# The start of a routed two-stage FFN kernel: first tile transposed uncentred, its row lookup taken ahead, and another order of gathers and matrix loads

## The chip, the cores and the metric

The kernel runs on one core of a Trainium2 chip. The metric is the device time of one execution in microseconds. TensorE is called PE here, VectorE DVE, ScalarE ACT, GpSimd POOL and SyncE SP, as in the profile. POOL issues the indirect DMAs (gathers and scatters of rows), SP the plain ones.

## The reference

2048 tokens of 512 numbers pass through two residual blocks. In the first one each token belongs to one of four experts by its id, and each expert has one 512x512 matrix, used for all three products:

```python
x = x + tanh(g_xattn[0]) * xattn(layernorm(x), ids, ctx, ctx, ctx)
x = x + tanh(g_ffn[0]) * ffn(layernorm(x), w1, w3, w2, wr)

def xattn(h, ids, Wg, Wu, Wd):           # per token's expert e
    e = minimum(clip(ids, 0, 24999) // 6250, 3)
    return (silu(h @ Wg[e].T) * (h @ Wu[e].T)) @ Wd[e].T

def ffn(x, w1, w3, w2, wr):
    gates, idx = top-2 of softmax(x @ wr.T), normalised
    h = silu(silu(x @ w1.T) @ w3.T) @ w2.T
    out = zeros_like(x)
    for k in range(2): out = out.at[idx[:, k]].add(gates[:, k:k+1] * h)
```

Wg, Wu and Wd are the same tensor, so z = h @ W.T is needed once, g = silu(z) * z, and y = g @ W.T. The second block adds into 8 rows only (the 8 routes), which is why its output is small.

## The kernel before

**Sorting the tokens.** The tokens are sorted by expert into 17 tiles ("passes") of 128 rows: 13 tiles that belong to one expert each (NF), and 4 mixed tiles in four groups of 32 rows. The list `order` gives the order in which they are worked. Lines 183 to 253 turn the ids into a place for every token: its tile (`inpass`) and its row in the tile (`lanes`). Lines 265 and 273 (`at_lane`) build one-hot matrices `atlane` (128 x 128 for each of 16 groups of tokens, the first 12 groups in one DVE instruction, the last 4 in another). Lines 266 to 272 build `what`, which holds for each of the 17 tiles the token's number where the token falls into that tile. 16 PE products (line 276) of the two give `tok`: for each row of each tile the number of its token. `from_row` (line 286) is the list of rows to gather, one column a tile. `which` (lines 287 to 300) tells for each tile the expert's offset in the matrices; `which0` (line 245) is the same for the first tile alone and is ready earlier. `row_tables()` (line 305) makes `to_row`, the rows to scatter to, and `first`, used much later.

`busy(n)` (line 198) issues n PE products of ones whose result nobody reads; there are 10 before the lookup and 21 behind it.

**Work on a tile.** `gather(p)` has POOL fetch the tile's rows x_p by an indirect DMA. `load(p)` has SP read the expert's offset from SBUF (`look_up`) and issue the 1 MB matrix load. `centre(p)` has DVE compute mean and variance (BATCH_NORM_STATS, BATCH_NORM_AGGREGATE) and h = x - mean. `scale(p)` has DVE compute 1/sqrt(variance) in nine small operations. `turn_in(p)` transposes h on PE (four 128x128 transposes) and copies it to SBUF on ACT (hT). `up(p)`: eight PE products z = hT x matrix, ACT's silu with the scale, DVE's product g (line 467). `turn_mid(p)` transposes g and copies it (gT). `down(p)`: eight PE products y, DVE's x + tanh(gate) * y in place (line 481), POOL's scatter to the output. `norms` and `turn_out` prepare the second block's input. For the first tile `first_in` stands in place of centre and turn_in: the same in two halves of 256 columns, so that PE and ACT can start on the first half.

**What sets the order.** Each engine works its instructions in the program's order, written out by hand (`manual_schedule`), and waits on semaphores for the others. The text at lines 836 to 874 is therefore the order of the start on each engine:

- DVE: the lookup, `row_tables`, first_in(0), scale 0, centre 1, scale 1, [g of tile 0], centre 2, scale 2, [g of tile 1], centre 3.
- POOL: gather 0, a copy of one entry of `which` into `held` (line 849), gathers 1 to 4, a copy of all later entries into `held` (line 854), then scatters and gathers in turn.
- SP: load 0 (offset from which0), load 1 (waits for the first copy into `held`), load 2 (waits for the second), the two gates, load 3, load 4, load 5, w1, wr and so on.
- PE: lookup, the 21 products of `busy`, transposes of tile 0, z_0 with the transposes of tile 1 put ahead of its last two products, z_1 with the transposes of g_0 ahead of its last two, the transposes of tile 2, y_0, the transposes of g_1, z_2.

Since SP reads the offsets of load 1 and on from `held`, such a load is issued only behind the gathers that stand ahead of its copy on POOL. Matrix tiles have 7 buffers, x tiles 5, hT 2, h 4.

Of the kernel before, what the change touches and what calls it, by code (L numbers as in the profile page):

```python
# [19 lines left out]
P = 128  # L20
# [5 lines left out]
def tile_gated_moe_ffn(  # L26
# [68 lines left out]
    positions = ExitStack()  # L95
    pos = positions.enter_context(tc.tile_pool(name="pos", bufs=1))
    on_the_way = {
        "lane", "atlane12", "atlane4", "passes", "what", "place", "over", "rank_in", "incl",
        "keep", "cum", "hot", "before", "later", "stepped", "behind", "ones", "place0", "number",
        "idt", "pad", "psum", "padded", "lanes", "inpass",  # L100
    }
# [30 lines left out]
    whole = ct_([P, 2, E], I32, "whole")  # L132
    nc.vector.memset(whole[:, 0, :], -P)
    nc.vector.memset(whole[:, 1, :], -Q)
    cut = ct_([P, 2 * E + 1], F32, "cut")
    nc.vector.memset(cut, 0.0)
    bounds = ct_([P, E - 1], F32, "bounds")
    for e in range(1, E):
        nc.vector.memset(bounds[:, e - 1 : e], BOUNDS[e - 1])

    steps = ct_([P, 2 * E - 1], F32, "steps")
# [6 lines left out]
        out=before, in_=before, pattern=[[-1, P]], compare_op=ALU.is_ge,  # L148
        fill=0.0, base=0, channel_multiplier=1,
    )  # L150
    H = 12
    lane = ct_([P, P, H], I16, "lane")
    nc.gpsimd.iota(lane, pattern=[[1, P], [0, H]], base=0, channel_multiplier=0)
    passes = ct_([P, NP, NJ], I16, "passes")
    nc.gpsimd.iota(passes, pattern=[[P, NP], [0, NJ]], base=0, channel_multiplier=0)

    number = ct_([P, NJ], F16, "number")
    nc.gpsimd.iota(
        number, pattern=[[1, NJ]], base=1, channel_multiplier=NJ,
# [3 lines left out]
    NU = NF + (NP - NF) * G  # L163
# [9 lines left out]
    ident = ct_([P, P], F32, "ident")  # L173
# [30 lines left out]
    incl = ct_([P, E, NJ], F32, "incl")  # L204
# [18 lines left out]
    rank_in = ct_([P, E, NJ], F32, "rank_in")  # L223
# [8 lines left out]
    over = ct_([P, E, NJ], F32, "over")  # L232
# [18 lines left out]
    nc.vector.tensor_single_scalar(lanes, padded, P - 1, op=ALU.bitwise_and)  # L251
    inpass = ct_([P, NJ], I16, "inpass")
    nc.vector.tensor_single_scalar(inpass, padded, -P, op=ALU.bitwise_and)
    atlane = [ct_([P, P, n], F16, f"atlane{n}") for n in (H, NJ - H)]

    def at_lane(h):
        j, n = (0, H) if h == 0 else (H, NJ - H)
        return nc.vector.tensor_tensor(
            atlane[h],
            lane[:, :, 0:n],  # L260
            lanes[:, j : j + n].unsqueeze(1).to_broadcast([P, P, n]),
            ALU.is_equal,
        )

    at_lane(0)
    what = ct_([P, NP, NJ], F16, "what")
    nc.vector.tensor_tensor(
        what, passes, inpass.unsqueeze(1).to_broadcast([P, NP, NJ]), ALU.is_equal
# [1 line left out]
    nc.vector.tensor_tensor(  # L270
        what, what, number.unsqueeze(1).to_broadcast([P, NP, NJ]), ALU.mult
    )
    at_lane(1)
    tok = ps_x.tile([P, NP], F32, tag="x", name="tok")
    for j in range(NJ):
        nc.tensor.matmul(
            tok, atlane[j // H][:, :, j % H], what[:, :, j], start=(j == 0), stop=(j == NJ - 1)
        )

    which = ct_([P, NU], I32, "which")  # L280
    later = ct_([P, 2 * E, NU], F32, "later")
    stepped = ct_([P, 2 * E - 1, NU], F32, "stepped")

    busy(21)
    from_row = ct_([P, NP], I32, "from_row")
    nc.vector.tensor_scalar(from_row, tok, -1.0, 0.0, ALU.add, ALU.max)
    nc.vector.tensor_tensor(
# [17 lines left out]
    def row_tables():  # L305

        pad = ct_([P, NP], F32, "pad")
        nc.vector.tensor_scalar(pad, tok, 1.0, float(4 * NT), ALU.is_lt, ALU.mult)
        nc.vector.scalar_tensor_tensor(to_row, tok, -1.0, pad, ALU.add, ALU.add)

        pads = ct_([P, E], F32, "pads")
        nc.vector.tensor_sub(pads, size[:, 2, :], num[:, 0, :])
        behind = ct_([P, E, NU - NF], F32, "behind")
        nc.vector.tensor_tensor(
            behind,
            later[:, E : 2 * E, NF:NU],
            pads.unsqueeze(2).to_broadcast([P, E, NU - NF]),
            ALU.mult,
        )
        psum = ct_([P, NU - NF], F32, "psum")  # L320
        nc.vector.tensor_reduce(psum, behind.rearrange("p e n -> p n e"), AX.X, ALU.add)
        nc.vector.tensor_sub(psum, place0[:, NF:NU], psum)
        nc.vector.tensor_scalar(
            first, psum, float(-(NB - 1) * TB), float(TB), ALU.add, ALU.min
        )
# [61 lines left out]
    def gather(p):  # L387
        xt = xp.tile([P, D], F32, tag="x", name=f"x_{p}")
        nc.gpsimd.indirect_dma_start(  # L389
            out=xt,  # L390
            out_offset=None,
            in_=x,
            in_offset=bass.IndirectOffsetOnAxis(ap=from_row[:, p : p + 1], axis=0),
        )
# [16 lines left out]

    def first_in(p):

        st = small.tile([P, 6], F32, tag="st", name=f"st_a{p}")
        nc.vector.bn_stats(st, xs[p])
        mvs[p] = small.tile([P, 2], F32, tag="mv", name=f"mv_a{p}")
        nc.vector.bn_aggr(mvs[p], st)
        hTs[p] = work.tile([P, KC * P], F32, tag="hT", bufs=2, name=f"hT_{p}")
        n = D // 2
        for i in range(2):  # L420
            h = work.tile([P, n], F32, tag="h", bufs=4, name=f"h_a{p}_{i}")
            nc.vector.tensor_scalar(
                h, xs[p][:, i * n : (i + 1) * n], mvs[p][:, 0:1], None, ALU.subtract
            )
            tp = ps_tp.tile([P, n], F32, tag="tp", name=f"tp_a{p}_{i}")
            for k in range(n // P):
                nc.tensor.transpose(tp[:, k * P : (k + 1) * P], h[:, k * P : (k + 1) * P], ident)
            nc.scalar.copy(hTs[p][:, i * n : (i + 1) * n], tp)  # L428
# [32 lines left out]
    def up(p, inside=None):  # L461
        z = ps_mm.tile([P, D], F32, tag="mm", name=f"z_{p}")
        expert_product(z, hTs.pop(p), p, inside)
        g = work.tile([P, D], F32, tag="g", bufs=2, name=f"g_{p}")
        rs = rss.pop(p)
        nc.scalar.activation(g, z, AF.Silu, scale=rs)  # L466
        nc.vector.scalar_tensor_tensor(g, z, rs, g, ALU.mult, ALU.mult)  # L467
        gs[p] = g

    def turn_mid(p):  # L470
        tp = transposed(gs.pop(p), f"g{p}")
        gT = work.tile([P, KC * P], F32, tag="gT", bufs=2, name=f"gT_{p}")
        nc.scalar.copy(gT, tp)  # L473
        gTs[p] = gT
# [358 lines left out]
            if r in (0, SHORT):  # L833
                step()

    row_tables()
    positions.close()
    ffp = ctx.enter_context(tc.tile_pool(name="ffp", bufs=1))
    held = ct_([P, NU], I32, "held")

    def look_up(i):
# [1 line left out]

    load(order[0])
    gather(order[0])
    one = slice(order[1], order[1] + 1)
    nc.gpsimd.tensor_copy(held[0:1, one], which[0:1, one])
    load(order[1])  # L850
    for i in range(1, 5):
        gather(order[i])
    rest = slice(order[1] + 1, NU)
    nc.gpsimd.tensor_copy(held[0:1, rest], which[0:1, rest])
    first_in(order[0])
    scale(order[0])
    centre(order[1])
    scale(order[1])
    load(order[2])
    nc.sync.dma_start(gates[:, 0:1], g_xattn.to_broadcast([P, 1]))  # L860
    nc.sync.dma_start(gates[:, 1:2], g_ffn.to_broadcast([P, 1]))
    load(order[3])
    up(order[0], inside=lambda: turn_in(order[1]))
    centre(order[2])
    scale(order[2])
    up(order[1], inside=lambda: turn_mid(order[0]))
    turn_in(order[2])
    centre(order[3])
# [94 lines left out]
```

## Time and profile before

| | us |
|---|---|
| median of three runs (lowest, highest) | 279.38 (278.96, 279.59) |
| profiled execution | 277.53 |
| its span, first to last instruction | 275.8 |
| PE busy | 266.6 (97%) |
| DVE busy | 148.7 (54%) |
| ACT busy | 69.3 (25%) |
| POOL busy | 39.3 (14%) |

How to read it: the span is cut by what the engines did, and a busy share of 97% says that PE is the bound nearly everywhere; the idle rest is at the start. The granted TensorE clock is 1.00 throughout. The chain of work that ended last is followed back from the last instruction; a name of a DMA in it is time from issue to landing. In the timeline, a line has start, duration, engine, line of the kernel, operation, output <- inputs, shape and count; in brackets stands the idle time of the engine ahead of it and what ended that. Neighbouring instructions of one line are merged into one line of the timeline.

The first 35 us go thus: the ids land at 2.56, the lookup products end about 8.9, gather 0 is issued at 9.35 and has landed at 12.87, matrix 0 is issued at 6.13, matrix 1 at 11.16, matrix 2 at 16.25. z_0 starts at 15.44, z_1 at 19.47, y_0 at 23.85, z_2 at 27.73.

### The profile page before, as it was taken

How to read it: one execution, taken by the hardware profiler on the slowest of the kernel's cores; microseconds unless marked ns; L12 is line 12 of the kernel's file. 1: busy time of each engine (PE TensorE's matmuls, PEld its weight loads, DVE VectorE, ACT ScalarE, POOL GpSimd, SP SyncE). 2: the span in 40 equal slices, each digit the busy share in tenths (PEclk: the TensorE clock that was granted, in tenths of full speed). 3: DMA queues.
4: the chain of work that ended last, by engine and by line, in shares of the span. 5: the costliest groups of instructions: out<-in, count | busy, mean ns of one | idle time of the engine just before them, and what ended most of it. 6: DMA issues, size and time to landing. Idle time of an engine off the chain costs nothing.

```text
span 275.8 us, 3562 instructions
## 1 busy us (share of the span) xinstructions
PE 266.6 (97%) x1173; PEld 125.4 (45%) x1173; DVE 148.7 (54%) x593; ACT 69.3 (25%) x134; POOL 39.3 (14%) x63
## 2 busy tenths in 40 slices
PE   5889999999999999999999999999999999999994
PEld 2445455544355454444344444534245444344362
DVE  6677877777888769918263481516253620711000
ACT  2022232232232231223143232312113233311120
POOL 6520122221122211211110010101010000000000
PEclk9999999999999999999999999999999999999999
DMA  0697998545669996697304084001000000000000
GB/s 1 217 354 277 408 402 334 173 155 206 228 225 402 389 409 258 173 398 264 112 26 166 2 312 180 38 0 40 0 12 2 0 0 1 0 0 2 0 0 2
DMA packets 20722, 42.54 MB, mean 154 GB/s; under 512 B 2143, under 2 KB 2207, under 8 KB 20704
## 3 DMA queue, kind: packets, MB, share of 16 engines
q1 hardware_dynamic: 17952, 33.66, 34.0%
q0 software_dynamic: 2720, 8.65, 8.3%
q8 instruction: 9, 0.15, 0.2%
q14 instruction: 9, 0.07, 0.1%
q10 hardware_dynamic: 32, 0.01, 0.0%
HBM read 38.10 MB, written 4.47 MB: 154 GB/s over the span
## 4 chain that ended last, share of the span: by engine, by line
PE 94%; DVE 2%; DMA 2%; issue 1%; ACT 0%; DVEq 0%
PE z L453 22%; PE y L453 21%; PE v L730 20%; PE X L622 10%; PE Y L622 5%; PE tp_f L380 3%; PE tp_a L380 3%; PE tp_g L380 3%; PE Z L622 2%; PE acc L742 1%; PE lg L699 1%; DMA x<-in_x_dram,from_row 1%; DMA idt<-in_ids_dram 1%; PE accT L758 1%; PE o L814 0%
## 5 line engine op out<-in xcount | busy, mean ns | idle before, releaser
L453 PE MATMUL z<-m,hT 128*32 128x512 f32 (+1 forms) x232 | 61.8, 595 | 0.2 <-ACT hT L428 0.2
L453 PE MATMUL y<-m,gT 128*32 128x512 f32 (+1 forms) x232 | 61.4, 594 | 0.0
L730 PE MATMUL v<-w,s 128*128 128x512 f32 (+1 forms) x136 | 57.3, 570 | 0.0
L730 PEld LDWEIGHTS v<-w,s 128*128 128x128 f32 x136 | 25.0, 190 | 27.2 <-issue 26.7
L453 PEld LDWEIGHTS z<-m,hT 128*32 128x32 f32 (+1 forms) x232 | 22.6, 146 | 29.5 <-issue 28.1
L453 PEld LDWEIGHTS y<-m,gT 128*32 128x32 f32 (+1 forms) x232 | 22.6, 146 | 27.8 <-issue 27.8
L482 POOL DMA_INDIRECT out_dram<-x,to_row x17 | 17.2, 1011 | 84.9 <-DVE x L481 82.7
L389 POOL DMA_INDIRECT x<-in_x_dram,from_row x17 | 16.7, 984 | 77.5 <-DVE h_a L401 22.9
L467 DVE SCALAR_TENSOR_TENSOR g<-z,rs_a,g 128x512 f32<-128x512 f32 x17 | 12.7, 750 | 27.1 <-ACT g L466 27.0
L466 ACT ACTIVATE g<-z,rs_a 128x512 f32<-128x512 f32 x17 | 11.7, 687 | 51.3 <-PE z L453 51.3
L481 DVE SCALAR_TENSOR_TENSOR x<-y,tg,x 128x512 f32<-128x512 f32 x17 | 12.7, 749 | 16.9 <-PE y L453 16.8
L738 ACT ACTIVATE s<-v 128x512 f32<-128x512 f32 (+1 forms) x17 | 9.7, 572 | 41.9 <-PE v L730 41.9
L515 ACT COPY hT<-tp_f 128x512 f32<-128x512 f32 x13 | 7.6, 587 | 43.5 <-PE tp_f L380 43.5
L340 DVE BATCH_NORM_STATS2 st_a<-x 128x6 f32<-128x512 f32 x16 | 11.0, 688 | 7.5 <-DMA x<-in_x_dram,from_row 7.5
L622 PE MATMUL X<-T,S 128*128 128x512 f32 x32 | 15.0, 592 | 0.0
L380 PEld LDWEIGHTS tp_f<-ident,h_f 128*128 128x128 f32 x68 | 8.2, 141 | 10.2 <-issue 10.2
L340 DVE BATCH_NORM_STATS2 st_f<-x 128x6 f32<-128x512 f32 x17 | 11.8, 695 | 0.6
L380 PEld LDWEIGHTS tp_a<-ident,h_a 128*128 128x128 f32 x64 | 7.7, 140 | 9.4 <-issue 9.1
L640 DVE TENSOR_TENSOR s<-X,c 128x512 f32<-128x512 f32 x4 | 2.8, 692 | 16.2 <-PE X L622 16.2
L473 ACT COPY gT<-tp_g 128x512 f32<-128x512 f32 x17 | 10.0, 586 | 5.3 <-PE tp_g L380 5.3
L380 PE MATMUL tp_f<-ident,h_f 128*128 128x128 f32 x68 | 10.4, 276 | 0.0
L380 PE MATMUL tp_g<-ident,g 128*128 128x128 f32 x68 | 10.2, 273 | 0.0
(165 smaller groups left out, 271.6 us busy)
## 6 DMA issues: line engine op xcount, KB each, us to landing
m<-in_ctxT_dram SPq DMA_DIRECT2D x29, 1024.0 KB
w<-in_w1T_dram SPq DMA_DIRECT2D x1, 1024.0 KB
w<-in_w3T_dram SPq DMA_DIRECT2D x1, 1024.0 KB
w<-in_w2T_dram SPq DMA_DIRECT2D x1, 1024.0 KB
x<-in_x_dram,from_row POOLq DMA_INDIRECT x17, 6.2
out_dram<-x,to_row POOLq DMA_INDIRECT x17, 6.1
wr<-in_wrT_dram SPq DMA_DIRECT2D x1, 64.0 KB
x_first<-out_dram SPq DMA_DIRECT2D x4, 4.0 KB
```

What stands on the lines that cost most here:

```text
L340: nc.vector.bn_stats(st, xt)
L380: nc.tensor.transpose(tp[:, k * P : (k + 1) * P], h[:, k * P : (k + 1) * P], ident)
L389: nc.gpsimd.indirect_dma_start(out=xt, out_offset=None, in_=x, in_offset=bass.IndirectOffsetOnAxis(ap=from_row[:, p : p + 1], axis=0),)
L453: nc.tensor.matmul(out_ps[i * n : (i + 1) * n, :], lhs[:, k * P + i * n : k * P + (i + 1) * n], m[:, k, :], start=(k == 0), stop=(k == KC ...
L466: nc.scalar.activation(g, z, AF.Silu, scale=rs)
L467: nc.vector.scalar_tensor_tensor(g, z, rs, g, ALU.mult, ALU.mult)
L473: nc.scalar.copy(gT, tp)
L481: nc.vector.scalar_tensor_tensor(xt, y, tg[:, 0:1], xt, ALU.mult, ALU.add)
L482: nc.gpsimd.indirect_dma_start(out=out, out_offset=bass.IndirectOffsetOnAxis(ap=to_row[:, p : p + 1], axis=0), in_=xt, in_offset=None, bou ...
L622: nc.tensor.matmul(out_ps, a[:, k, c * P : (c + 1) * P], bb[:, k, :], start=start and k == 0, stop=k == 1, skip_group_check=True,)
L730: nc.tensor.matmul(v, s1[:, k, c_b + t * P : c_b + (t + 1) * P], w3[:, k, c0 : c0 + n], start=(k == 0), stop=(k == KC - 1),)
L738: nc.scalar.activation(s2, v, AF.Silu)
```

## The change

1. *Lookup of the first tile ahead.* The one-hot matrices are built in three instructions of 6, 6 and 4 groups instead of two of 12 and 4. A column `what0` for the first tile alone is made first, and 16 products of one column each give `tok0`, from which `from_row0` is made; only then come `what` for all tiles and the 16 full products. `which1` (the second tile's offset) is made from the cuts directly, as which0 was. `busy` has 3 products behind the first lookup and 10 behind the second.
2. *First tile transposed as it comes.* `first_in` transposes x_0 itself instead of x_0 - mean. The mean is subtracted afterwards: DVE sums each row (`total`), a PE product spreads the sums along the transposed tile's columns (`spread`, in PSUM), and DVE computes hT = raw - spread / 512 in two halves. Mean and variance of tile 0 follow on DVE.
3. *Another order of gathers and loads.* Gather 0 reads `from_row0`; gathers 1 and 2 read `from_row`; all later ones read `rows_on`, a copy of it that DVE makes behind `first_in`. POOL's copy for load 1 stands behind gather 0 as before, now with `which1`; the copy for all later loads stands behind gather 2 instead of gather 4.
4. *Another order on DVE.* centre 1 stands ahead of scale 0, centre 2 ahead of g_0, scale 1 and scale 2 behind g_0, and `row_tables` behind scale 2 and ahead of g_1.

```diff
-    H = 12
+    H = 6
...
+    what0 = ct_([P, NJ], F16, "what0")
+    nc.vector.scalar_tensor_tensor(what0, inpass, 0.0, number, ALU.is_equal, ALU.mult)
+    at_lane = []
+    for i, j in enumerate(range(0, NJ, H)):
+        n = min(H, NJ - j)
+        at = ct_([P, P, n], F16, f"atlane{i}")
+        nc.vector.tensor_tensor(
...
+            ALU.is_equal,
+        )
+        at_lane.extend(at[:, :, k] for k in range(n))
+    tok0 = ps_x.tile([P, 1], F32, tag="x", name="tok0")
+    for j in range(NJ):
+        nc.tensor.matmul(
+            tok0, at_lane[j], what0[:, j : j + 1], start=(j == 0), stop=(j == NJ - 1)
+        )
+    busy(3)
+
+    start1 = ct_([P, 2 * E - 1], F32, "start1")
+    nc.vector.scalar_tensor_tensor(
+        start1, cut[:, 1 : 2 * E], float(P), steps, ALU.is_le, ALU.mult
+    )
+    which1 = ct_([P, 1], I32, "which1")
+    with nc.allow_low_precision("whole numbers below 4096"):
+        nc.vector.tensor_reduce(which1, start1, AX.X, ALU.add)
+    from_row0 = ct_([P, 1], I32, "from_row0")
+    nc.vector.tensor_scalar(from_row0, tok0, -1.0, 0.0, ALU.add, ALU.max)
...
-    busy(21)
+    busy(10)
...
-            in_offset=bass.IndirectOffsetOnAxis(ap=from_row[:, p : p + 1], axis=0),
+            in_offset=bass.IndirectOffsetOnAxis(
+                ap=from_row0
+                if p == order[0]
+                else (from_row if p in order[1:3] else rows_on)[:, p : p + 1],
+                axis=0,
+            ),
...
-        st = small.tile([P, 6], F32, tag="st", name=f"st_a{p}")
-        nc.vector.bn_stats(st, xs[p])
...
+        raw = work.tile([P, KC * P], F32, tag="h", bufs=4, name=f"raw_{p}")
         for i in range(2):
...
+                nc.tensor.transpose(tp[:, k * P : (k + 1) * P], xs[p][:, c : c + P], ident)
+            nc.scalar.copy(raw[:, i * n : (i + 1) * n], tp)
+        total = small.tile([P, 1], F32, tag="total", name="total")
+        nc.vector.tensor_reduce(total, xs[p], AX.X, ALU.add)
+        spread = ps_y.tile([P, P], F32, tag="y", name="spread")
+        nc.tensor.matmul(spread, total.to_broadcast([P, P]), ident, start=True, stop=True)
+        hTs[p] = work.tile([P, KC * P], F32, tag="hT", bufs=2, name=f"hT_{p}")
+        for i in range(2):
+            half = slice(i * n, (i + 1) * n)
+            nc.vector.scalar_tensor_tensor(
+                hTs[p][:, half].rearrange("p (k t) -> p k t", t=P),
+                spread.unsqueeze(1).to_broadcast([P, n // P, P]),
+                -1.0 / D,
...
+        mvs[p] = moments(xs[p], f"a{p}")
...
-    row_tables()
-    positions.close()
-    ffp = ctx.enter_context(tc.tile_pool(name="ffp", bufs=1))
...
+    rows_on = ct_([P, NP], I32, "rows_on")
     load(order[0])
     gather(order[0])
-    one = slice(order[1], order[1] + 1)
-    nc.gpsimd.tensor_copy(held[0:1, one], which[0:1, one])
+    one, rest = slice(order[1], order[1] + 1), slice(order[1] + 1, NU)
+    nc.gpsimd.tensor_copy(held[0:1, one], which1[0:1, :])
     load(order[1])
-    for i in range(1, 5):
-        gather(order[i])
-    rest = slice(order[1] + 1, NU)
+    gather(order[1])
+    gather(order[2])
     nc.gpsimd.tensor_copy(held[0:1, rest], which[0:1, rest])
     first_in(order[0])
+    nc.vector.tensor_copy(rows_on, from_row)
+    gather(order[3])
+    gather(order[4])
+    centre(order[1])
     scale(order[0])
-    centre(order[1])
-    scale(order[1])
+    centre(order[2])
     load(order[2])
...
     load(order[3])
     up(order[0], inside=lambda: turn_in(order[1]))
-    centre(order[2])
+    scale(order[1])
     scale(order[2])
+    row_tables()
+    positions.close()
+    ffp = ctx.enter_context(tc.tile_pool(name="ffp", bufs=1))
     up(order[1], inside=lambda: turn_mid(order[0]))
```

More of the change, by code (lines that the diff above doesn't have):

```diff
@@ L97, in tile_gated_moe_ffn @@
     on_the_way = {
-        "lane", "atlane12", "atlane4", "passes", "what", "place", "over", "rank_in", "incl",
+        "lane", "atlane0", "atlane1", "atlane2", "passes", "what", "place", "over", "rank_in", "incl",
         "keep", "cum", "hot", "before", "later", "stepped", "behind", "ones", "place0", "number",
-        "idt", "pad", "psum", "padded", "lanes", "inpass",
+        "idt", "pad", "what0", "psum", "padded", "lanes", "inpass",
     }
@@ L253, in tile_gated_moe_ffn @@
     nc.vector.tensor_single_scalar(inpass, padded, -P, op=ALU.bitwise_and)
[L254 to L259, printed above, removed]
+    what0 = ct_([P, NJ], F16, "what0")
[5 more added lines that the diff above has]
+        nc.vector.tensor_tensor(
+            at,
             lane[:, :, 0:n],
@@ L263, in at_lane @@
         )
-    at_lane(0)
+        at_lane.extend(at[:, :, k] for k in range(n))
[14 more added lines that the diff above has]
+    nc.vector.tensor_scalar(from_row0, tok0, -1.0, 0.0, ALU.add, ALU.max)
     what = ct_([P, NP, NJ], F16, "what")
@@ L272, in tile_gated_moe_ffn @@
     )
-    at_lane(1)
     tok = ps_x.tile([P, NP], F32, tag="x", name="tok")
@@ L276, in tile_gated_moe_ffn @@
         nc.tensor.matmul(
-            tok, atlane[j // H][:, :, j % H], what[:, :, j], start=(j == 0), stop=(j == NJ - 1)
+            tok, at_lane[j], what[:, :, j], start=(j == 0), stop=(j == NJ - 1)
         )
@@ L412, in first_in @@
     def first_in(p):
-        st = small.tile([P, 6], F32, tag="st", name=f"st_a{p}")
-        nc.vector.bn_stats(st, xs[p])
-        mvs[p] = small.tile([P, 2], F32, tag="mv", name=f"mv_a{p}")
-        nc.vector.bn_aggr(mvs[p], st)
-        hTs[p] = work.tile([P, KC * P], F32, tag="hT", bufs=2, name=f"hT_{p}")
         n = D // 2
+        raw = work.tile([P, KC * P], F32, tag="h", bufs=4, name=f"raw_{p}")
         for i in range(2):
[L421 to L424, printed above, removed]
             tp = ps_tp.tile([P, n], F32, tag="tp", name=f"tp_a{p}_{i}")
             for k in range(n // P):
-                nc.tensor.transpose(tp[:, k * P : (k + 1) * P], h[:, k * P : (k + 1) * P], ident)
-            nc.scalar.copy(hTs[p][:, i * n : (i + 1) * n], tp)
+                c = i * n + k * P
+                nc.tensor.transpose(tp[:, k * P : (k + 1) * P], xs[p][:, c : c + P], ident)
[11 more added lines that the diff above has]
+                -1.0 / D,
+                raw[:, half].rearrange("p (k t) -> p k t", t=P),
+                ALU.mult,
+                ALU.add,
+            )
+        mvs[p] = moments(xs[p], f"a{p}")
     def load(p):
```

## The prediction

> **What bounds the kernel now.** I read the page's shares, then the chain of work that ended last, then the timeline of the first 30 us. The chain is TensorE:
>
> ```profile
> PE 94%; DVE 2%; DMA 2%; issue 1%; ACT 0%; DVEq 0%
> ```
>
> The 6% that are not PE lie ahead of the first z product (and a sliver at the end). In order of time that chain runs:
>
> ```profile
> 7.85 1.01 PE tok L276 x16
> ...
> 8.88 0.19 DVE from_row L286
> 9.07 0.28 issue
> 9.35 3.52 DMA x<-in_x_dram,from_row
> ...
> 15.44 2.84 PE z L453 x6
> ```
>
> From 15.44 on TensorE never stops, so any time by which the first z starts earlier is kept, unless something stops PE later. Only the first 35 us matter. What limits there is read from the timeline (start, duration, engine, line):
>
> ```profile
> 6.23 0.96 DVE L258 TENSOR_TENSOR atlane<-lane,lanes 128x1536 f16<-128x1536 int16 x1
> 10.25 0.17 DVE L308 TENSOR_SCALAR pad<-tok 128x17 f32<-128x17 f32 x1
> 11.49 0.29 DVE L323 TENSOR_SCALAR first<-psum 128x16 int32<-128x16 f32 x1
> 18.12 0.60 PE L380 MATMUL tp_a<-ident,h_a 128*128 128x128 f32 x4
> 24.34 0.75 DVE L467 SCALAR_TENSOR_TENSOR g<-z,rs_a,g 128x512 f32<-128x512 f32 x1
> 27.29 0.60 PE L380 MATMUL tp_g<-ident,g 128*128 128x128 f32 x4
> ```
>
> Row tables (L308 to L323) sit in DVE's wait for the first gather and cost nothing. The second tile's g is done at 25.09; PE turns it at 27.29: 2.2 us of slack on DVE, which the change spends.
>
> **The change part by part** (all times in us from the span's start; rows are those of the timeline). *Lookup.* inpass ends at 6.19 and its reader starts at 6.23; what0 is like the 16-wide rows (0.16), so atlane can start at 6.31. 1536 columns took 0.96 and 512 took 0.42, so 768 take 0.55; each operation starts 0.08 before its forerunner ends: 6.31, 6.78, 7.25, the last ending 7.67. PE spends 0.99 on 16 lookups (0.053 each, last one 0.2 long), and the last four can load only after 7.67: done about 8.2. from_row0 0.18, POOL 0.29 later (as 9.06 to 9.35): **gather 0 at 8.69 instead of 9.35**. The three busy() (0.22 each) lie in PE's wait for what and cost nothing; behind the second lookup ten (2.24) follow instead of 21, so PE is free at 12.1.
>
> *Landing.* Alone, gather 0 took 3.5 us to land. Now its descriptors (1.13 us of POOL) are ready at 9.82, when matrix 0 still moves: all its 528 packets lie before 10.9. Between "nothing in the way" (8.69+3.5 = 12.2) and "only after matrix 0" (10.83 + the 2.0 which before lay between that and 12.87, so 12.8) I take L = 12.45.
>
> *First tile.* Before, from landing to z: 15.44−12.87 = 2.57. Now: 0.02, a 512-wide reduce (no row; from below the 203-wide one's 0.53, from above that stretched to 512, 1.33; I take BATCH_NORM_STATS over the same tile, 0.69), 0.13 to PE, spread 0.28, 0.04, half of hT (512 took 0.75 and 128 took 0.35: 0.48), 0.04: 1.68. ACT's raw copy is done at L+0.95, hidden by the reduce. **z_0 at 14.13, a lead of 1.31.** With 1.33 for the reduce the lead would be 0.67 and all that follows on DVE 0.64 later.
>
> *What is late next.* After the spread (1.16 behind L) DVE does, in this order, the two halves of hT, statistics of x_0 (two operations), rows_on, then centre 1. Start to start: 1.16+0.40+0.40+0.73+0.11+0.08 = 2.88 after L. Call B the time at which centre 1 begins: 15.33 (before: 16.37, behind scale 0, which now comes after). Now count on from B to PE's transposes of g_1, start to start with the durations that the same operations have before: centre 1.34, scale 1.76, centre 1.34, g_0 0.67, scale 1.77, scale 1.76, row tables 1.45 (10.25 to 11.78, less overlap), g_1 0.75, 0.13 to PE: 10.97. So PE gets g_1 at B+10.97 where it had it at 27.29: **gain = 16.32−B**, 0.99 at B = 15.33, and never over the lead of 1.31. The row tables' move alone costs 1.45 here; before they were covered by the wait for the gather. The needs in between hold: h_a of tile 1 at B+1.42 = 16.75 against PE's 14.13+2.68 (15.44 to 18.12 before); g_0 at B+5.19+0.13 = 20.65 against 20.8.
>
> *Gathers and matrices.* gather 1 now waits for the whole lookup: what runs behind from_row0 (8.32 to 9.01), PE 9.06 to 10.05, from_row 10.25, POOL 10.53 (before 10.83). Matrix 1 is released by the copy behind gather 0: 10.49 (before 11.16). Gather 2 follows at 11.81 (before 12.11), the copy for matrix 2 and on at 12.8 and matrix 2 at 13.45 (before 16.25); gates, matrices 3 to 5 and w1 follow it in SP's queue, equally earlier, and were in time before. Gathers 3 and 4 wait on POOL for rows_on, so start about 15.6 and 16.9 (13.36, 14.62); at 6 to 7 us each they land by 24, and DVE reads x_3 after 26. Scatter 0 stands behind them, due only at 28.8. What matters is x_1 at B and x_2 at B+3.10. Before:
>
> ```profile
> 10.83 0.97 POOL L389 DMA_INDIRECT x<-in_x_dram,from_row  x1 [0.15 <-issue]
> 12.11 0.95 POOL L389 DMA_INDIRECT x<-in_x_dram,from_row  x1 [0.31 <-issue]
> ```
>
> They landed 5.0 and 7.4 us after these starts (15.8, 19.5). With 5.0 again x_1 is there at 15.53, B = 15.55, gain 0.77. x_2's packets came when matrix 1's ended, so it either keeps 7.4 us (19.2: gain 19.42−19.22 = 0.2, as g_1 follows x_2 by 7.87) or moves with matrix 1 by 0.67 (18.83: 0.57); gathers 3 and 4 no longer share the engines with it, matrix 2 now does. Nearest is matrix 1's row; I take 18.7: **gain 0.7**.
>
> *Sum.* 277.53 (span 275.8) − 0.7 = 276.8 for the profiled execution; the three runs' median, 279.38, stands 1.85 above that one, so 278.7. Behind g_1 DVE catches up: g_2 is ready at 32.9 and PE asks at 34.8, h_f of tile 0 at 32.2 against 34.4. From there on the order is as before.
>
> [...] Before, while gather 1 went, both queues moved:
>
> ```profile
> q1 hardware_dynamic: 242, 0.50, 59.8%
> q0 software_dynamic: 80, 0.26, 33.2%
> ```
>
> (13.2 to 15.6). But for the gather started at 68.21, beside a matrix issued at 68.24, the window 69.2 to 72.7 has one queue only:
>
> ```profile
> q1 hardware_dynamic: 440, 0.90, 79.4%
> ```
>
> Not one gather packet in 3.5 us; it landed after 6.7. [...]
>
> The clock: PEclk is 1.00 from 12 to 16 us although PE was busy 0.38 and 0.43 us of 13 to 15, so I charge nothing for the two thin microseconds ahead of the new z_0. [...]
>
> **Rivals.**
>
> *Slower: gather 1 falls wholly behind matrix 1.* Matrix 1's issue would end at 10.88 and gather 1's descriptors at 11.50, 0.62 later. Before it was 11.55 and 11.80 (0.25), and they shared. At 59.8 (issue ends 60.14, gather 60.17) they shared too, landing 5.4. At 68.2 (68.61 and 69.19, 0.58) the gather waited, 6.7. So the change moves gather 1 to the wrong side. Then x_1 lands at 10.53+6.7 = 17.2, B = 17.25, the gain is −0.9: 280.3. It decides from B = 16.32, x_1 at 16.3. Against it: gather 0 now stands ahead of matrix 1 on the engines and may hold it until gather 1 is ready.
>
> *No difference: x_2 keeps its 7.4 us.* DVE stands at statistics of tile 2 until 19.2, the gain is 0.2: 279.2. For it: matrix 2, issued 2.8 us earlier, takes the place of gathers 3 and 4.
>
> *More: nothing is late.* x_1 by 15.3 and x_2 by 18.4: 0.99, or up to the lead of 1.3 if DVE's row tables shrink in the gaps: 278.1 to 278.4.
>
> **The numbers.** Forecast (0.3 to 0.9 gained) 0.37, more 0.12, no difference 0.18, slower 0.33. A difference under 0.2% (0.56 us) is about what measuring can't tell from none. Of the forecast 0.34 lies above 0.56, so faster 0.46; within, 0.03+0.18 and 0.01 of the slower: 0.22; slower 0.32. The likeliest case alone spans 278.5 to 279.1; the range takes in the lead (278.0) and the rival with 0.1 for its bound (280.4).
>
> **What would show it.** gather 0 near 8.7, landing by 12.5; first z near 14.1; statistics of tile 1 at 15.3 to 15.6 and not ended by a DMA; transposes of tile 1 without a wait; a wait of DVE for x_2 of 0 to 0.3; then PE waiting for g_1 some 0.5 us, with row tables directly ahead of it on DVE. Wrong if DVE's statistics of tile 1 wait past 16.3, if PE shows a granted clock under 1, or if PE waits for a matrix.

## The result and the profile after

The changed kernel took 279.04 us (median of 12 runs, 277.0 to 279.88), the kernel before on the same chip 278.95 (12 runs, 278.19 to 279.8): ratio 0.9994, 95% interval 0.9975 to 1.0013. A second measurement gave 279.05 against 278.94, ratio 1.0002 (0.9985 to 1.0019). So there is no difference that can be measured. The profiled execution took 279.21 (span 277.5).

The chain of work that ended last, from the page of the changed kernel and, below, two of its pieces in order of time (start, us, what):

```profile
PE 85%; DMA 9%; DVE 3%; issue 1%; SPq 1%; POOL 0%
```

```profile
11.70 7.34 DMA x<-in_x_dram,from_row
...
79.43 15.11 DMA m<-in_ctxT_dram
```

Before, the chain held DMAs only ahead of the first z product. Now it passes through two more: gather 2 (x_2), and the fourth matrix of a mixed tile, long after the start. The start itself, in the timeline of the changed kernel:

```profile
8.70 1.25 POOL L406 DMA_INDIRECT x<-in_x_dram,from_row  x1 [4.44 <-DVE what L285]
...
12.38 0.69 DVE L446 TENSOR_REDUCE total<-x 128x1 f32<-128x512 f32 x1 [0.95 <-DMA x<-in_x_dram,from_row]
...
13.12 0.49 PE L448 MATMUL spread<-ident,total 128*128 128x128 f32 x2
...
14.19 2.84 PE L485 MATMUL z<-m,hT 128*128 128x512 f32 x6 [0.59 <-DVE hT L452]
...
15.46 0.69 DVE L357 BATCH_NORM_STATS2 st_a<-x 128x6 f32<-128x512 f32 x1
...
18.56 0.30 PEld L485 LDWEIGHTS z<-m,hT 128*128 128x128 f32 x2 [0.87 <-ACT hT L432]
...
19.06 0.69 DVE L357 BATCH_NORM_STATS2 st_a<-x 128x6 f32<-128x512 f32 x1 [0.40 <-DMA x<-in_x_dram,from_row]
...
25.94 0.74 DVE L499 SCALAR_TENSOR_TENSOR g<-z,rs_a,g 128x512 f32<-128x512 f32 x1
...
26.82 0.63 PE L397 MATMUL tp_g<-ident,g 128*128 128x128 f32 x4 [0.17 <-DVE g L499]
```

Gather 0 starts at 8.70, x_0 is there at about 12.36 (its first reader starts at 12.38; the trace lacks most records of this landing), z_0 starts at 14.19, tile 1's statistics at 15.46 with no DMA in the brackets. The first bracket with a DMA on DVE behind that is tile 2's, at 19.06. PE turns g_1 at 26.82, 0.47 earlier than before (27.29). Its lead was 1.25 at z_0 and 0.82 at the transposes of g_0 (21.30 against 22.12). Some 0.2 of that went at z_1 (the 18.56 line; PEld is the load of PE's weights). The bracket names hT of tile 1, but that was ready at 18.29; z_1 starts at 18.59, 0.13 behind the landing of matrix 1 at 18.46. What is left at g_1 is still there at 93.4 us. Then, PE in the profile of before and of the changed kernel:

```profile
93.84 3.64 PE L453 MATMUL z<-m,hT 128*32 128x512 f32 x32
...
102.31 1.95 PE L699 MATMUL lg<-hT,wr 128*32 128x128 f32 x64
104.19 3.70 PE L453 MATMUL z<-m,hT 128*128 128x512 f32 x8
```

```profile
93.41 4.79 PE L485 MATMUL z<-m,hT 128*32 128x512 f32 x32
...
103.02 1.68 PE L731 MATMUL lg<-hT,wr 128*32 128x128 f32 x43
105.05 0.90 PE L731 MATMUL lg<-hT,wr 128*32 128x128 f32 x21 [0.35 <-issue]
105.88 3.70 PE L485 MATMUL z<-m,hT 128*128 128x512 f32 x8
```

The z products of the mixed tile (32 of them) last 4.79 instead of 3.64, and the 64 short products of the router (lg) end 2.86 behind their start instead of 1.88. The timeline of the weight loads shows what ended the first stop:

```profile
94.58 0.16 PEld L485 LDWEIGHTS z<-m,hT 128*32 128x32 f32 x8 [1.02 <-DMA m<-in_ctxT_dram]
```

From 0.43 ahead, the changed execution is 1.69 behind the first profile of before, and it stays so to the end. The record does not say on which chip that first profile was taken.

### The profile page after: what moved, and what is told of

Same layout as the page of the kernel before. It is cut to its first block, busy times and chain, and to the rows that moved or that the text cites. A ratio compares the mean times of both kernels' runs of the same rounds, so it can differ in the third digit from the quotient of the medians.

```text
span 277.5 us, 3585 instructions
## 1 busy us (share of the span) xinstructions
PE 268.7 (97%) x1183; PEld 125.8 (45%) x1183; DVE 149.1 (54%) x600; ACT 69.3 (25%) x134; POOL 38.9 (14%) x63
## 4 chain that ended last, share of the span: by engine, by line
PE 85%; DMA 9%; DVE 3%; issue 1%; SPq 1%; POOL 0%
PE v L762 20%; PE y L485 18%; PE z L485 16%; PE X L654 10%; DMA m<-in_ctxT_dram 5%; PE Y L654 5%; DMA x<-in_x_dram,from_row 3%; PE tp_f L397 3%; PE Z L654 2%; PE tp_g L397 2%; PE tp_a L397 2%; PE lg L731 2%; PE idle L200 2%; PE acc L774 1%; DMA idt<-in_ids_dram 1%
## 5 line engine op out<-in xcount | busy, mean ns | idle before, releaser
L485 PE MATMUL z<-m,hT 128*32 128x512 f32 (+1 forms) x232 | 63.0, 596 | 0.8 <-DVE hT L452 0.6
L514 POOL DMA_INDIRECT out_dram<-x,to_row x17 | 17.2, 1010 | 86.7 <-DVE x L513 84.8
L406 POOL DMA_INDIRECT x<-in_x_dram,rows_on x14 | 13.8, 986 | 72.8 <-DVE h_a L423 34.4
L513 DVE SCALAR_TENSOR_TENSOR x<-y,tg,x 128x512 f32<-128x512 f32 x17 | 12.7, 750 | 18.7 <-PE y L485 18.7
L357 DVE BATCH_NORM_STATS2 st_a<-x 128x6 f32<-128x512 f32 x17 | 11.7, 687 | 7.4 <-DMA x<-in_x_dram,rows_on 6.9
```

The costliest lines, as they stand in the source:

```text
L406: nc.gpsimd.indirect_dma_start(out=xt, out_offset=None, in_=x, in_offset=bass.IndirectOffsetOnAxis(ap=from_row0 if p == order[0] else (fro ...
L485: nc.tensor.matmul(out_ps[i * n : (i + 1) * n, :], lhs[:, k * P + i * n : k * P + (i + 1) * n], m[:, k, :], start=(k == 0), stop=(k == KC ...
L513: nc.vector.scalar_tensor_tensor(xt, y, tg[:, 0:1], xt, ALU.mult, ALU.add)
L514: nc.gpsimd.indirect_dma_start(out=out, out_offset=bass.IndirectOffsetOnAxis(ap=to_row[:, p : p + 1], axis=0), in_=xt, in_offset=None, bou ...
```

## The experiments

ACT's copy of g_1's transpose ("gT of tile 1", 27.93 in the first profile of before) is the mark for the start in all that follows.

**1. The same two kernels again, and with room for the matrices.** The edit for room, the same in both:

```diff
-    mp = ctx.enter_context(tc.tile_pool(name="mp", bufs=7))
+    mp = ctx.enter_context(tc.tile_pool(name="mp", bufs=8))
...
-        if i == 7:
+        if i == 10:
             w3 = load_w(w3T, "w3")
-            w2 = load_w(w2T, "w2")
+        if i == 14:
+            w2 = mp.tile([P, KC, D], F32, tag="m", name="w2")
+            nc.sync.dma_start(w2, w2T.rearrange("(k p) f -> p k f", p=P))
```

The kernel before, unchanged:

> The kernel before, once more and unchanged, for a second profile and for what a measurement against itself gives. Ratio 1.000 within 0.003. Both theories: first z at 15.4, g_1 turned at 27.3. Theory A (the time lost behind 93 us comes from matrix landings that scatter from one execution to the next in both kernels): this second profile may show a wait of PE for the mixed tile's matrices near 94 or a gap near 104, up to 1 us each. Theory B (the changed kernel alone pays there, since its PE comes 0.43 earlier to matrices that land no earlier): no wait there, as in the first profile.

The changed kernel, unchanged:

> The changed kernel unchanged. Both theories: gather 0 at 8.7, first z at 14.2, g_1 turned at 26.8 (0.47 ahead of before). Theory A: the losses near 94 and 104 (1.1 and 1.0 in the first profile) have other sizes or are absent; the time lies 0.0 to 0.5 us under before in the median. Theory B: a loss of 0.4 or more near 94 again, the time equal to before.

The kernel before with room:

> The kernel before with 8 matrix buffers instead of 7, w3 loaded three tiles later, and w2 loaded at the end into a matrix buffer, so that the matrices used at 94 and 104 us land some us before they are asked for. Theory A: waits there vanish and the time falls to the level of the best executions, 277.3 to 278.0, ratio to before 0.995 to 0.998. Theory B: the kernel before has no wait there to lose, ratio 1.000 within 0.002.

The changed kernel with room:

> The changed kernel with the same room for matrices. Both theories: the 0.4 to 0.5 won at g_1 reaches the end, since nothing behind takes it back: 0.45 under before_roomy. Theory A: 276.9 to 277.6. Theory B: 278.4 to 278.6, that is 0.45 under before. If it equals before_roomy, the gain is lost at some other place that both theories miss.

Against 278.94 for the kernel before on that chip (35 runs): before again 279.12, ratio 1.0 (0.9985 to 1.0016); changed again 279.05, 1.0002 (0.9985 to 1.0019); before with room 278.06, 0.9971 (0.9954 to 0.9989); changed with room 277.85, 0.9969 (0.9954 to 0.9985). Gains at gT of tile 1, each against its partner: 0.43 (first pair), 0.72, 0.26. So the changed start wins in each pair, though which execution stands beside which is arbitrary (27.39 to 28.51 before, 27.13 to 27.79 changed), and room brings 0.3% to either kernel. Both theories had the changed kernel with room 0.45 under the kernel before with room. That did not come: it is 0.2 by the medians, with ratios that can't be told apart, and the two profiles end even (spans 275.9 and 275.8), 0.26 ahead at gT of tile 1 and 0.27 more lost in lg. The second profile of before has a stop that the first has not:

```profile
94.42 3.64 PE L453 MATMUL z<-m,hT 128*32 128x512 f32 x32
...
102.89 1.67 PE L699 MATMUL lg<-hT,wr 128*32 128x128 f32 x47
104.92 0.42 PE L699 MATMUL lg<-hT,wr 128*32 128x128 f32 x3 [0.37 <-issue]
105.67 0.68 PE L699 MATMUL lg<-hT,wr 128*32 128x128 f32 x14 [0.32 <-issue]
106.28 3.70 PE L453 MATMUL z<-m,hT 128*128 128x512 f32 x8
```

Its burst lasts 1.5 longer than 1.88, without any semaphore: "issue" is PE waiting for nothing that the profile shows. So the first profile of before is not typical of this chip: its 277.53 lies under all 12 runs shown beside the changed kernel, and among those of the two faster chips of experiments 2 and 3 (277.04 to 278.9 and 276.93 to 278.41), from one of which it may come. The theory that only the changed kernel pays behind the start falls: the burst of lg is 1.5 longer in the second profile of before, 1.0 and 1.7 in the two of the changed kernel (with room 0.5 and 0.8). Why room helps the kernel before is not shown: no profile of it has a wait at the mixed tile that room could take away, only its stop in lg is shorter with room, in one execution.

**2. The burst of lg in two.** Half of the router's products are put ahead of the first X product (of the second block's first layer) instead:

```diff
-        lgs = [logits(b, half) for half in range(2)]
+        lg = logits(b, 0)
...
-        lts[b] = [turned(b, half, lg) for half, lg in enumerate(lgs)]
+        lts[b] = [turned(b, 0, lg)]
...
+        lts[b].append(turned(b, 1, logits(b, 1)))
         yield from first_layer(b)
```

The last of the four kernels also has the row tables moved:

```diff
+    up(order[1], inside=lambda: turn_mid(order[0]))
     row_tables()
     positions.close()
     ffp = ctx.enter_context(tc.tile_pool(name="ffp", bufs=1))
-    up(order[1], inside=lambda: turn_mid(order[0]))
```

The kernel before with it:

> The kernel before with the router's products (lg) of the second half moved from just behind those of the first half, ahead of the z product at about 104, to just ahead of the first X product at about 112: two bursts of 32 instead of one of 64, nothing else. In the traces so far PE stops inside the burst for 'issue' after 44 to 50 of the 64 products in five of six executions (0.5 to 1.2 us in all), and what the start had won or the rest had lost came together there. Theory 1 (a burst of more than some 45 of these short products outruns PE's own instruction stream): no gap over 0.2 us inside either burst, and the times fall by 0.5 to 1.5 us, to 277.4 to 278.4. Theory 2 (the gaps are only something of that one place in time, such as full DMA queues, whatever the burst): gaps stay in the first burst, same time as before, 278.9.

The changed kernel with it:

> The same move of half of lg in the changed kernel. Theory 1: no gap in the bursts, 277.0 to 278.0, and 0.3 to 0.5 us below the kernel before with the same move, since the start's gain is then carried through. Theory 2: as the changed kernel, 279.0. Theory 3 (the gain is lost again at the matrix of the mixed tile near 94, which is still in place): gaps in lg gone, but PE waits for that matrix about as much longer as it comes earlier, and the two moved kernels come out the same.

The kernel before with room and with it:

> The kernel before with room for the mixed tiles' matrices (eight slots, w3 and w2 loaded later) and with half of lg moved. Theory 1: 277.2 to 277.8, up to 0.8 below the 278.06 of the roomy one alone. Theory 2: 278.1.

The changed kernel with room, with it, and with the row tables behind g_1:

> The changed kernel with that room, half of lg moved, and the row tables on DVE put from ahead of g of the second tile to just behind it, so that g_1 no longer stands behind 1.45 us of them. Locally: g_1's transposes begin at about 26.5 instead of 26.8 (PE waits for them no more than 0.1 us), row tables done by about 28, still ahead of the scatter of the first tile at 28.8. Over all, theory 1: 276.6 to 277.2, some 0.5 to 0.8 below the kernel before with the same room and move. Theory 2 or 3: within 0.3 of it.

They ran on another chip, where the kernel before takes 277.73 (24 runs). In the order above: 278.72, ratio 1.0039 (1.0025 to 1.0052); 279.23, 1.0054 (1.0036 to 1.0073); 279.2, 1.0054 (1.0034 to 1.0074); 278.58, 1.0021 (1.0003 to 1.0038). There is no gap over 0.2 us in any of the bursts, as the first theory had it, yet the times rise. The move has a price of its own, in the kernel before with the split (PE, then DVE):

```profile
117.84 1.55 PE L622 MATMUL X<-hT,w 128*128 128x512 f32 x3 [0.33 <-DVE lt L710]
```

```profile
117.48 0.31 DVE L710 STREAM_TRANSPOSE lt<-lg 128x128 f32<-128x128 f32 x1
```

The second X needs the PSUM buffer of the moved lg, and DVE reads that one only at 117.48, behind all its work for the norms. And since the kernel before is 1.2 us faster here than on the first chip, there may have been little to win. The split kernels can't tell whether smaller bursts or the other chip took the gaps away. The row tables' move won 0.18: with x_1 at 16.7 in both changed kernels, gT of tile 1 is at 28.25 with the tables ahead of g_1 and at 28.07 with them behind it.

Each changed kernel also has a partner here. Without room it is 0.5 behind its partner by the medians; it is 0.28 ahead at gT of tile 1, its mixed tile is 0.41 late, and the spans are 277.5 and 277.6, near what theory 3 had. With room it is 0.6 ahead, as theory 1 had it. In that pair's profiles it is 0.40 ahead at gT of tile 1 and 0.41 still at 104 us and up to the second X at 118, so what was won at the start came through the mixed tile. Then the kernel before alone waits 0.99 for DVE's read of the moved lg, and the distance is 1.25. The timed 0.6 is therefore not the start's alone.

**3. Matrix 1 released later.** In both kernels x_1 comes at scattered times (statistics of tile 1 begin at 15.9 to 17.2 in five profiles of the order before, 15.5 to 16.7 in five of the changed). The copy that releases matrix 1 is put behind gather 1, then behind gather 2, the row tables behind g_1:

```diff
+    gather(order[1])
     nc.gpsimd.tensor_copy(held[0:1, one], which1[0:1, :])
     load(order[1])
-    gather(order[1])
     gather(order[2])
```

> The changed kernel with the copy that releases matrix 1 put behind gather 1 instead of behind gather 0 (and the row tables behind g_1, so that they do not hide the effect). In the ten profiles so far x_1 landed between 15.4 and 17.1 in both kernels, by the last of its 16 engines, because matrix 1's packets stand ahead of its own on some of them; PE then waited up to 1.5 us for tile 1. Theory 1 (matrix 1 is what holds gather 1 up): x_1 lands by 14.5 (start 10.4 and the 3.5 to 4 us that a gather takes with nothing ahead of it), tile 1's statistics begin without a DMA wait near 15.3, PE waits at tile 1's transposes under 0.2 us, and matrix 1 lands about 1 us later (18.2 to 18.5, where PE asks near 18.2). All: 0.3 to 1.2 us below the changed kernel of the same chip. Theory 2 (the scatter of x_1 has another cause): x_1 still between 15.4 and 17.1, same time.

> The same with that copy behind gather 2, just ahead of the one for the later matrices. Theory 1: x_1 by 14.3, x_2 by 16, no DMA wait at all on DVE until tile 3; matrix 1 is issued near 12.9 instead of 10.7 and lands 17 to 18.5, matrix 2 behind it at 20 to 21 against PE's 22. If matrix 1 lands past 18.3, PE waits for it at z_1 and the gain is smaller by that. All: 0.5 to 1.5 us below the changed kernel. Theory 2: x_1 as late as ever, matrix 1 later for nothing, 0 to 1 us above the changed kernel.

On a third chip (before: 277.44, 20 runs): 278.53, ratio 1.0039 (1.0021 to 1.0056), and 279.12, 1.007 (1.0045 to 1.0095). x_1 landed at 13.9 and 13.7, so matrix 1 is what holds gather 1 up (on which of the engines, the traces don't tell). But matrix 1 landed at 20.4 and 19.95, not by 18.5, and PE stood for it. Timeline and stretches of the first of the two (of a stretch: its length, then busy time of PE, PEld, DVE, ACT, POOL, granted clock, DMA share, GB/s):

```profile
15.31 0.69 DVE L357 BATCH_NORM_STATS2 st_a<-x 128x6 f32<-128x512 f32 x1
...
20.53 4.51 PE L485 MATMUL z<-m,hT 128*128 128x512 f32 x6 [2.02 <-DMA m<-in_ctxT_dram]
```

```profile
18.00:20.50 2.50, 0.51 (x2) 0.00 (x0) 2.33 (x8) 0.96 (x2) 0.00 (x0) 1.00 1.05 380
20.50:25.00 4.50, 4.47 (x8) 1.85 (x9) 3.14 (x19) 0.00 (x0) 0.00 (x0) 0.62 0.83 283
```

The 2.02 us of waiting are not all: the granted clock was 0.62 in the next stretch (in the trace 0.50 from 21.45 on for 3.4 us, and 1.00 around it), and six products took 4.51 instead of 2.84. This execution was the slowest of its 12 (280.99). In the second of the two PE waited 1.81, the clock stayed at 1.00 and the six took 2.81. gT of tile 1 is at 30.68 and 28.54, where the changed kernel and its variants have 27.1 to 28.3. So what x_1 wins is lost again at z_1, and more. The changed kernel itself was not timed on this chip; against the kernel before, these two orders lose 0.4% and 0.7%, and the change lost nothing on the first chip. As far as that goes, gather 1 and matrix 1 at one time is the best of the three orders.

**4. Is a time at the start still there at the end?** The first lane comparison five times over:

```diff
-        nc.vector.tensor_tensor(
-            at,
+        for _ in range(5 if i == 0 else 1):
+            nc.vector.tensor_tensor(
+                at,
...
```

> The changed kernel with the first of the three lane comparisons (768 columns, 0.55 us, 0.47 from start to start) done five times over: everything from the lookup on begins 1.9 us later, nothing else. It asks whether a time won or lost at the start is still there at the end. Kept (the prediction's step): first z 1.7 to 1.9 later, g of the mixed tile behind lg 1.5 to 2 later than in the changed kernel, all 1.5 to 2 us above it (ratio near 1.006). Swallowed (the loads of matrices near 94 or PE's stops in lg set the time there, whenever PE comes): the offset shrinks to under 1 at 108 us, and all is under 1 us above the changed kernel (ratio under 1.004).

On the third chip: 280.79, ratio 1.0114 (1.0095 to 1.0132), which is 3.35 above the kernel before. The delay came out larger than meant:

```profile
12.16 3.96 PE L200 MATMUL idle<-ones 128*128 128x512 bf16 x10
15.96 0.60 PE L444 MATMUL tp_a<-ident,x 128*128 128x128 f32 x4
...
17.36 2.84 PE L486 MATMUL z<-m,hT 128*128 128x512 f32 x6 [0.58 <-DVE hT L453]
```

PE had stood 1.67 us for the lookup, and the ten products that nobody reads then took 0.40 each instead of 0.23 (2.33 for ten in the changed kernel); the transposes of x_0 stood behind them although it had landed at 14.5. So z_0 is 3.2 later than in the profile of the changed kernel shown above. Of that 3.0 is there at gT of tile 1 (30.45 against 27.49). Nothing is swallowed: against the first profile of before the offset is 2.5 at gT of tile 1, 3.2 from the mixed tile on and 3.2 at the end. And again, on PE:

```profile
96.37 4.33 PE L486 MATMUL z<-m,hT 128*32 128x512 f32 x32
...
105.52 1.95 PE L732 MATMUL lg<-hT,wr 128*32 128x128 f32 x64
```

No stop in lg, but the mixed tile is late by 0.69, with PE 3 us later than in the changed kernel. So that wait does not come from PE being early. The run shows that time lost at the start is kept; of time won it shows nothing.

**5. What is late at the mixed tile.** The nine profiles with seven matrix buffers, by order ("changed" takes in its variants of experiments 2 to 4). PE asks for the fourth matrix (start of the 32 z products) 14.0 us after its issue in all nine, since the issue follows PE too:

| order | issue to landing | last engine behind the last but one | the 32 z products |
|---|---|---|---|
| before (3) | 12.66, 13.58, 13.78 | 0.17, 0.45, 0.48 | 3.64, 3.64, 3.64 |
| changed (6) | 15.10, 14.22, 14.39, 14.70, 14.60, 14.68 | 1.05, 0.93, 1.23, 0.88, 0.90, 1.22 | 4.79, 3.88, 4.05, 4.34, 4.25, 4.33 |

The changed order pays 0.24 to 1.15 there, on all three chips; the order before (profiled on two of them) nothing. A landing is taken here as the last of the 16 updates of the matrix's semaphore, read as one for each of 16 DMA engines, and in the changed order the last comes 0.9 to 1.2 behind the fifteenth: by this reading it is one engine that is late. One thing that differs in the traces is a packet of an instruction queue (the "fetch" below). The DMA queues from 80 to 93 us, before and changed (packets, MB, share):

```profile
q14 instruction: 3, 0.02, 0.4%
```

```profile
q14 instruction: 4, 0.03, 0.7%
q8 instruction: 1, 0.02, 0.5%
```

The q8 packet is 16 KB and takes 1.0 to 1.2 us. It comes at 84 to 92 us, ahead of the landing, in all six of the changed order, and at 94.6 to 94.9, behind the landing, in all three of the order before. The lag of the last engine is about its length. The change adds some 20 PE instructions at the start. From the two lengths I argue that the matrix had to stand behind this packet on one DMA engine. No run shifted the fetch alone, and the traces don't tell on which engine a packet ran, so this is not shown. With room, the kernel before has had the fetch early too (85.8), so the number of instructions alone doesn't set when it comes. And in the changed kernel with room one matrix landed at 83.48, its last engine 2.01 behind, ahead of that kernel's fetch at 85.31: such a lag has another cause too.

**6. Room without the split.** The changed kernel with room and the row tables behind g_1:

> The changed kernel with room for the mixed tiles' matrices and the row tables behind g_1; the router's burst whole again. Reading of the runs so far: in the changed kernel without that room the z products of the mixed tile (32 of them, 3.64 us when nothing stops them) took 3.88 to 4.79 in all six profiles, on three chips, and 3.64 in all three of the order before; so the start's 0.3 to 0.7 us go there, and the stops inside lg are a matter of the chip (in all five profiles of the unsplit burst on the chip with the 278.9 us median, in none of the three on the chip with 277.4). Theory 4 (the gain of the start reaches the end as soon as the mixed tile's matrix is not late): mixed z 3.64 here, g_1's transposes 0.3 to 1 us ahead of the kernel before, and 0.4 to 1.0 us below the kernel before on a chip without stops in lg (ratio 0.9965 to 0.9985), 0.9 to 1.5 below on the chip with them (0.995 to 0.997). Theory 5 (something else in the changed kernel costs time too): mixed z 3.64, and within 0.3 us of the kernel before on a chip without stops.

On the first chip: 278.09 (12 runs) against 278.87 (17), ratio 0.9982 (0.9966 to 0.9998). Its profiled execution (276.74, span 275.0):

```profile
24.47 0.74 DVE L499 SCALAR_TENSOR_TENSOR g<-z,rs_a,g 128x512 f32<-128x512 f32 x1
```

```profile
93.06 3.64 PE L485 MATMUL z<-m,hT 128*32 128x512 f32 x32
...
101.53 1.96 PE L731 MATMUL lg<-hT,wr 128*32 128x128 f32 x64
103.41 3.70 PE L485 MATMUL z<-m,hT 128*128 128x512 f32 x8
```

g_1 is ready 1.5 us earlier and PE no longer waits for it; gT of tile 1 is at 27.15, 0.78 ahead of the first profile of before. No matrix is late, lg does not stop, and the offset is 0.78 at the end too: in this execution the gain is carried through whole. It is the fastest of its 12 runs, and the profile that it is set against has no stop in lg either. My sentence that lg stops in every unsplit execution of this chip falls with it. The timed gain, 0.8 by the medians and 0.5 by the ratio, is at or under the lower end of what theory 4 gave for this chip. And the kernel before with room alone stands 0.9 below the kernel before (278.06, experiment 1). So with room in both kernels the timing shows no gain of the start. The three kernels with room and the whole burst beat the two without it and are not to be told apart (0.9982, 0.9969 and 0.9971), so the row tables' move is seen in the profiles alone.

## Why the prediction was right, and where it was not

- *Lookup, landing, first tile*: right within 0.1 us at each mark. Gather 0 8.70 (8.69), landing 12.36 (12.45), the unknown reduce 0.69 as taken from the statistics' row, z_0 14.19 (14.13). One term was too small: spread, two products in the trace, took 0.49 instead of 0.28. From landing to z_0 it was 1.83 and not 1.68, and part of that was made up by the early landing.
- *What is late next*: right in the main. Statistics of tile 1 at 15.46 (15.33 to 15.55), not ended by a DMA; row tables directly ahead of g_1; PE waits for g_1, though for 0.17 and not for some 0.5. It had lost 0.43 of its lead by the transposes of g_0: those of tile 1 stood 0.17 for h_a, and z_1 some 0.2 for matrix 1. A wait for a matrix was one of the prediction's own signs of being wrong; it left g_1 as it was, which follows x_2 on DVE. That x_1 was in time is luck too: it landed at 15.43, and in other executions the statistics came up to 1.2 later. The slower rival's mechanism, gather 1 behind matrix 1, is real (experiment 3: x_1 at 13.9 and 13.7 with matrix 1 released later), but x_1 comes as late in the order before, where no run parted the two.
- *x_2*: the rival's rule held, not mine. It kept its 7.4 us (7.34) and was there at 19.04 instead of 18.7. The gain at g_1 is 0.47, not 0.7; the mean of the five pairs at gT of tile 1 is 0.42 (0.43, 0.72, 0.26, 0.28, and 0.40 with the row tables moved).
- *The step that failed* is "any time by which the first z starts earlier is kept, unless something stops PE later. Only the first 35 us matter", and with it "From there on the order is as before". The order is as before, but the fourth matrix of a mixed tile had 1.34 us to spare in the one profile that I read (0.40 and 0.22 in the two others), and takes 0.4 to 2.4 us longer in the changed kernel's executions. Of the 0.43, 0.72 and 0.28 won at the start in the three pairs with seven buffers, 1.15, 0.24 and 0.41 are paid there; in the first pair lg takes another 1.0, in the second 0.2. With that matrix in time the sentence holds to 0.01 us in the profiles of experiment 6 and of the pair with room in experiment 2. Those are single executions. The medians do not show it: with room in both kernels of experiment 1 they lie 0.2 apart, and the profiles end even, since lg took the rest. Why that matrix lands later in the changed order stays open.
- *The base.* The sum was made against an execution without stops in lg. The 1.85 us to the median I carried over as a constant. The second profile of before is 2.1 longer than the first, and 1.5 of that is the stop in lg; whether the first one is of the same chip is not on record. That did no harm to the difference, but it hid that every execution has another end.
- *The result* lies in the range, nearest to the time of "no difference" (279.2) and for half of its reason: x_2 was late as it said, which left 0.4 and not 0.2, and the rest went, in the profile, at the mixed tile and in lg, which no rival named. A gain of 0.4 is also less than these intervals can show, so the timing alone would not have told either. That the time lies in the range is thus no proof of the forecast gain: 0.7 was forecast, and the medians are 0.1 apart, the other way.
- *Clock.* The two thin microseconds ahead of z_0 cost nothing, as forecast: from 12.4 to 14.2 us PE was busy for 1.12 of 1.80, the granted clock was 1.00, and the first six products of z_0 took 2.84, as before. In the first order of experiment 3 it fell to 0.50, 0.92 behind the end of 2.02 us of waiting, with PE busy for 0.51 of the 2.50 us from 18.00 to 20.50; in the second it stayed at 1.00 behind 1.81 us of waiting. Two executions show no more than that.

## What to carry to other kernels

A margin read from one profile is one draw: ask for every transfer that the rest of the kernel waits for how much it has to spare, and count one like the 1.34 us here as a loss that waits to happen, whatever the change. An edit at the start can be right to 0.1 us and still be paid back 70 us later, so follow the offset against the old profile along the whole span before trusting or blaming the edit. Where a gain is smaller than the scatter, make the difference large (delay the start on purpose) to see whether time there counts at all.

## What the hardware showed that was not expected

- PE stops inside a burst of 64 short products (1.9 us for all), mostly after 43 to 50 of them, for 0.3 to 0.6 us at a time, with no semaphore; the burst gets 0.5 to 1.7 longer. It was so in five of the seven profiles with the whole burst that stand beside a median of 278.9 to 279.4 for the kernel before (one of the two without is the first profile of before, whose chip is not on record), and in none of the three on the third chip. The second burst of the same kind, at 210 to 216 us, does not stop (1.88 to 1.89 in seven profiles), with a DMA share of 0.01 from 210 to 216 us in the first profiles of before and of the changed kernel, against 1.04 from 100 to 106 us in both. No instruction packet lies between 98 and 105 us in these two. What PE waits for stays open; that it outruns its instructions, the first theory of experiment 2, no trace shows.
- The same kernel before takes 278.9, 277.7 and 277.4 us on three chips.
- The granted clock reads 0.62 where z products slowed (experiment 3), but 1.00 where ten bf16 products took 0.40 us each instead of 0.23 (experiment 4, 12.16 to 16.12). In that trace the first record of the clock starts at 15.52, so the 1.00 ahead of it is no measurement: see where the records begin. In the first profile of before that is at 6.23, and the same products stood 0.43 apart ahead of it and 0.22 behind it.
- A DMA's landing is that of its last semaphore update, read as that of its last engine: x_1's, up to 1.8 us behind the last but three, and a matrix's, 1.2 behind the last but one (2.0 in the changed kernel with room).
